# Copying k beside q[dst] out of PSUM, and making a block's products one block earlier, in a graph attention kernel on one core

## The chip, the core and the metric

The kernel runs on one core of a Trainium2 chip. The metric is the device time of one execution in microseconds; that of the kernel before is the median of three runs. The profile is of one further execution, whose own time is given beside its span.

## The reference, cut to what matters

One layer of attention over a graph's edges, with a layer norm ahead of it and a residual behind it. There are 12,500 nodes and 212,500 edges with 128 features each, sorted by destination, and 8 heads of 16.

```
h = maximum(layernorm(x), 0)
q = (h @ Wq.T + bq).reshape(N, 8, 16)
k = (edge_attr @ Wk.T + bk).reshape(E, 8, 16)
v = (h @ Wv.T + bv).reshape(N, 8, 16)
qs, qd = q[src], q[dst]
in_m, out_m, diag_m = sum(qs * k, -1), sum(qd * k, -1), sum(qs * qd, -1)
score = (segment_softmax(in_m / 4, dst) + segment_softmax(out_m / 4, dst)
         + segment_softmax(diag_m / 4, dst)) * edge_weight ** lam
out = x + leaky_relu(segment_sum(score[..., None] * v[dst], dst) @ Wo.T + bo, 0.1)
```

## The kernel before, in words

The edges are cut into blocks of 512, each of four times 128 edges (one edge to a partition). A block belongs to one of five strands s and to a group t; the loop of the main part (L1534 and following) runs over the 415 blocks g in the order s = g % 5, t = g // 5. All five engines have their own queue, and a helper, `pin`, ties each instruction to the one before it on its engine, so that every engine works in the order in which the program is written. That order is laid out by hand, and a late instruction holds up all that stands behind it on its engine.

What is done for a block g, with the line that does it:

- `gather` (L696, POOL): four indirect DMAs fetch the 512 rows q[src] into a tile qq. They are issued LOOK = 23 blocks ahead into QQ = 25 buffers. Each of the four is tied to a product of PE of the iteration before (`behind`), so that it does not start earlier.
- `one_hots` (L1177, L1178, ACT): from the places of the edges' destinations within a window of nodes, a one-hot matrix oh in bf16.
- `spread_q` (L1201, PE): four matmuls of oh with the window's rows of q and its rest, into kq_ps, a PSUM tile of 128x1024 floats with two buffers. One half becomes q[dst]; the other half takes a first term of k (the bias).
- `turn` (L1183, PE, and L1185, ACT): transposes the edge features into eT_ps (one buffer), and ACT copies them to eT in SBUF.
- `project` (L1190, PE, and L1194, ACT): multiplies eT by Wk and adds it onto k's half of kq_ps; then ACT copies the half with q[dst], 128x512, into qd in SBUF.
- `logits` (L1215, L1216, L1220, DVE): the product of qd with k (one input in SBUF, one in PSUM), the products of qq with both halves of kq_ps (again one in PSUM), and behind the blocks of s = 0, 2 and 4 a reduce over each head.

So kq_ps goes free when DVE's second product has read it, and the next but one block's `spread_q` on PE needs that buffer. In iteration g, PE and ACT make block g + 1's `spread_q` and `project`, block g + 2's `turn` and block g + 3's `one_hots`, and DVE makes block g's `logits`.

Once a group, spread over the five iterations, stands the softmax along each strand: scans on DVE (L1274, L1279, L1292), transposes on PE (L1241, L1366), powers (L1376 on DVE, an exponential L1377 on ACT, L1387 on DVE), the selection of rows (L1402 on PE, L1405 and L1406 on ACT) and the sums onto rows (L1417 on PE, L1423 on ACT). Node work and further terms of q (L1097 to L1148, L1305 to L1321) are put between. SP issues the loads: the edge features of a group (`fetch_edges`, ea, 1.28 MB) at s = 0 for the group after, the places (relb, L641) at s = 2 and the far rows (L627) at s = 3, each for the group after the next, window rows (L650) and the stores of sums (L1434).

Outside the loop, L861 and L958 belong to the start, where the q rows and the order of the edges are made, and ends_ab is a tile for the last sums at the tail.

Of the kernel before, what the change touches and what calls it, by code (L numbers as in the profile page):

```python
# [7 lines left out]
F32 = mybir.dt.float32  # L8
# [464 lines left out]
def ordered_path(ctx: ExitStack, tc: tile.TileContext, flag, x, src, dst, edge_attr, edge_weight,  # L473
# [19 lines left out]
    nc = tc.nc  # L493
    N, F = x.shape
    E = src.shape[0]
    P = 128
    NI = -(-N // P)
    NP = P * NI
    BE, JN = 512, 4
# [11 lines left out]
    H3 = 3 * HEADS  # L511
# [75 lines left out]
    worst = consts.tile([RW, 1], F32, name="worst")  # L587
    LEAD, RAW, AHEAD = 3, 15, 11
    raw_i = consts.tile([P, LEAD, S, JN], I32, name="raw_i")
    LOOK, QQ, BEGIN = 23, 25, 12  # L590
    end = S * G
    edges = ctx.enter_context(ExitStack())
    gath = edges.enter_context(tc.tile_pool(name="gath", bufs=QQ))
# [4 lines left out]
    def pin(inst):  # L598

        engine = str(inst.ins.engine)  # L600
        if engine in pinned:
            tc.add_manual_dep(inst.ins, pinned[engine], mybir.DependencyInfo(
                mybir.DependencyClass.NoSync, mybir.DependencyReason.DATA), reason="in order")
        pinned[engine] = inst.ins.name
        return inst
# [8 lines left out]
    qqs, st, eas, behind, base_v, places = {}, {}, {}, {}, {}, {}  # L614
# [124 lines left out]
    with tc.tile_pool(name="prep", bufs=1) as prep, \  # L739
# [44 lines left out]
        rest = E - (RW - 1) * RC  # L784
# [280 lines left out]
    class Nodes:  # L1065
# [39 lines left out]
        def turn(self, to):  # L1105
            for b in range(self.n):
                pin(nc.tensor.transpose(to[:, b, :], self.h[:, b, :], ident))
            if self.hT is None:
                self.hT = fin.tile([P, JN, P], F32, name="hT")
            pin(nc.scalar.copy(self.hT[:, :self.n], to[:, :self.n]))  # L1110
# [50 lines left out]
    with tc.tile_pool(name="work", bufs=2) as work, \  # L1161
            tc.tile_pool(name="scan", bufs=2) as scan, \
            tc.tile_pool(name="ps", bufs=1, space=PSUM) as ps:
        kqs, eTs, qds, ohs, lTs, prods = {}, {}, {}, {}, {}, {}

        def banks_of(g):

# [4 lines left out]
        def one_hots(g):  # L1172

            if g < end:
                oh = ohs[g] = work.tile([K3, BE], BF, name="oh", bufs=5)
                d = places[g // S][:K3, g % S, :]
                pin(nc.scalar.activation(d, d, AF.Abs, bias=before[:K3]))  # L1177
                pin(nc.scalar.activation(oh, d, AF.Relu, bias=1.0, scale=-1.0))  # L1178
# [9 lines left out]
        def project(g):  # L1188
            for j in range(JN):
                pin(nc.tensor.matmul(kqs[g][:, j, 1, :], eTs[g][:, j, :], wk, start=False,  # L1190
                                     stop=(j % 2 == 1)))
            del eTs[g]
            qds[g] = work.tile([P, JN, F], F32, name="qd")
            pin(nc.scalar.copy(qds[g], kqs[g][:, :, 0, :]))  # L1194

        def spread_q(g):

            s, win = g % S, st[g // S]["win"]
            kq = banks_of(g)
            for j in range(JN):  # L1200
                pin(nc.tensor.matmul(kq[:, j].rearrange("p i f -> p (i f)"),  # L1201
                                     ohs[g][:, j * P:(j + 1) * P], win[:, s:S + 1:S - s, :],
                                     start=(j % 2 == 0), stop=False))
            del ohs[g]

        def logits(g):
            s, t = g % S, g // S
            if s == 0:
                lTs[t] = scan.tile([P, JN, S, H3], F32, name="lT", bufs=3)
            alone = t == G - 1 and s > 2  # L1210
            lo = s if alone else max(0, s - 1 + s % 2)
            if s == lo:
                prods[0] = work.tile([P, JN, 2, 3, F], F32, name="prod", bufs=1)
            prod = prods[0][:, :, s - lo]
            pin(nc.vector.tensor_mul(prod[:, :, 2, :], qds[g], kqs[g][:, :, 1, :]))  # L1215
            pin(nc.vector.tensor_mul(prod[:, :, 0:2, :],  # L1216
                                     qqs[g][:, :, None, :].to_broadcast([P, JN, 2, F]),
                                     kqs[g]))
            if s % 2 == 0 or alone:
                pin(nc.vector.tensor_reduce(  # L1220
                    lTs[t][:, :, lo:s + 1, :].rearrange("p j s c -> p j (s c)"),
                    prods[0][:, :, :s + 1 - lo].rearrange("p j s i (h d) -> p j (s i h) d", d=DIM),
                    AX.X, ALU.add))
            del kqs[g], qds[g], qqs[g]

        last = {}
        ends_ab = scan.tile([P, len(rest) * JN, 2, 2 * H3], F32, name="ends_ab", bufs=1)
        for i in range(2):
            ends_t.append(scan.tile([K4, P], BF, name=f"ends_t{i + 2}", bufs=1))
            nc.vector.memset(ends_t[-1][0:1, :], 1.0)  # L1230
# [1 line left out]
        def small(shape, name):  # L1232
            return ps.tile(shape, F32, name=name, tag="small", bufs=3)
# [286 lines left out]

        products = str(mybir.EngineType.PE)
        leaving, last_pair = pairs[G - 3], pairs[G - 1]
        fetch_rows(0)
        fetch(1)
        fetch_places(1)
# [5 lines left out]
        turn(1)  # L1531
        one_hots(1)
        one_hots(2)
        for g in range(end):  # L1534
            s, t = g % S, g // S
            nodes_before(t, s)
            gather(g + LOOK)
            if s == 0:
                fetch_edges(t + 1)
            if g + 1 < end:  # L1540
                spread_q(g + 1)
                behind[g + 1, 0] = pinned[products]
                project(g + 1)
                behind[g + 1, 1] = pinned[products]
            if g + 2 < end:
                turn(g + 2)
                behind[g + 1, 2] = pinned[products]
            if s == 4:
                later(weigh_powers, t - 2)
            logits(g)  # L1550
            if s == 3:
                later(powers, t - 2)
            one_hots(g + 3)
            if s == 0:
                if t > 0:
                    turn_logits(t - 1)
                later(select, t - 2)
                later(spread_far, t - 2)
            elif s == 1:
                later(scan_on, t - 1)  # L1560
                later(scan_back, t - 2)
                if t == 1:
                    logits_few()
            elif s == 2:
                if t == G - 2:
                    show_ends(G - 1)
# [12 lines left out]
            if t == G - 3 and 0 < s < 3:  # L1579
                select(G - 2 + s)  # L1580
            if t == G - 2 and s == 4:
                show_ends(G)
            if t == G - 1 and s == 0:
                select(G - 2)
            if t == G - 1 and s == 4:
                show_ends(G - 2)
            behind[g + 1, 3] = pinned[products]
            nodes_between(t, s)
            other_terms(t, s)
            if g == 12 * S:  # L1590
                examine()
            begin_rest(g - (end - BEGIN))
            if g == end - 2:
                hold(rest[0], True)
            if g == end - 1:
                last_pair.turn(small([P, JN, P], "node_ps"))
                more_banks()
            if g < S:
                of = [u for u in range(NU) if g in parts_of(u)]
                pin(nc.scalar.dma_start(  # L1600
                    sums[g][of[0] * UN:(of[0] + len(of)) * UN].rearrange(
                        "(n p) i c -> p n (i c)", p=P),
                    blank[:, None, :].to_broadcast([P, 2 * len(of), 2 * 2 * H3])))
# [28 lines left out]
        hold(rest[1])  # L1632
        last_pair.turn(small([P, JN, P], "node_ps"))
        last_pair.project_o(small([P, JN, F], "node_ps"))
        for r, of in enumerate(rest):
            of.load_sums(ends_ab[:, r * JN:r * JN + of.n], of.more)
        last_pair.take_larger()
# [88 lines left out]
```

## Time and profile before

| what | value |
|---|---|
| median of 3 runs | 2659.78 us (2658.79 to 2670.84) |
| the profiled execution's own time | 2642.74 us |
| its span | 2640.9 us |
| mean granted clock of PE | 0.786 |
| DMA, mean over the span | 135 GB/s |

In the profile, PE is the matmuls, PEld the weight loads beside them, DVE, ACT, POOL and SP the other engines. A group of instructions is given by line, engine, operation, and "out<-in" by the tiles' names, with how often it ran, its busy time, the mean of one in ns, and the idle time of its engine in front of it with what ended that. "Issue" is idle time in which the engine waited for nothing that the profile shows; "remote" is a releaser that it cannot name. A row of the list of waits has the total in us, how often, and the longest. A row of the timeline has the start and the duration in us, and in brackets the idle time before it. The matmuls' ends are modelled.

### The profile page before, as it was taken

The numbers are of one execution on the slowest core, as the hardware profiler recorded it, in microseconds if no ns is written. First come the engines' busy times: TensorE is split into PE (matmuls) and PEld (weight loads), VectorE is DVE, ScalarE is ACT, GpSimd is POOL, SyncE is SP. The second block draws the span as 40 slices with busy tenths as digits, with TensorE's granted clock in tenths as the row PEclk, the third lists the DMA queues.
The fourth block names the chain that finished last, engine by engine and source line by source line (L and its number), as shares of the span: only waits on it lengthen the run. The fifth ranks groups of instructions, "written<-read, shape, count | busy, mean of one in ns | idle before, by whom it ended". The sixth has DMA issues, their size and how long they took to land.

```text
span 2640.9 us, 34648 instructions
## 1 busy us (share of the span) xinstructions
PE 1657.0 (63%) x9986; PEld 1406.9 (53%) x9986; DVE 2002.2 (76%) x2205; ACT 1422.5 (54%) x2742; POOL 1587.3 (60%) x1678
## 2 busy tenths in 40 slices
PE   5655656565665566666666666565666666666677
PEld 4544545454555455555555565454555555555665
DVE  6656777777787777777878777777877787778896
ACT  6644555455555555555555555555554555555572
POOL 6666666666666666666666666666666666666200
PEclk9876777778777887877878777878877787778786
DMA  8464444444444444444444444444444444444431
GB/s 235 143 202 130 132 121 121 145 131 121 129 147 132 131 132 148 140 132 130 134 139 144 126 134 144 144 122 130 146 139 129 124 145 139 120 126 133 122 91 53
DMA packets 306303, 355.74 MB, mean 135 GB/s; under 512 B 118433, under 2 KB 225899, under 8 KB 305795
## 3 DMA queue, kind: packets, MB, share of 16 engines
q1 hardware_dynamic: 238340, 238.99, 29.8%
q0 software_dynamic: 53184, 108.92, 15.0%
q10 hardware_dynamic: 14580, 5.53, 0.8%
q8 instruction: 82, 1.34, 0.2%
q14 instruction: 117, 0.96, 0.1%
HBM read 321.41 MB, written 31.85 MB: 134 GB/s over the span
## 4 chain that ended last, share of the span: by engine, by line
PE 31%; ACT 22%; another core or an unknown queue 17%; issue 14%; DVE 10%; DMA 0%; DVEq 0%; POOL 0%; ACTq 0%; SPq 0%; POOLq 0%
PE kq_ps L1190 11%; PE w_ps L1417 6%; PE kq_ps L1201 5%; ACT qd L1194 4%; ACT eT L1185 4%; PE eT_ps L1183 4%; ACT relb L1177 4%; DVE lT L1220 3%; DVE prod L1216 3%; ACT oh L1178 2%; PE node_ps L1115 2%; ACT sel L1406 2%; ACT sel L1405 2%; ACT back L1377 1%
## 5 line engine op out<-in xcount | busy, mean ns | idle before, releaser
L696 POOL DMA_INDIRECT qq<-q_table,src_i x1600 | 1517.2, 948 | 852.1 <-issue 368.8
L1190 PE MATMUL kq_ps<-wk,eT 128*128 128x128 f32 x3320 | 627.3, 348 | 677.0 <-ACT eT L1185 478.3
L1190 PEld LDWEIGHTS kq_ps<-wk,eT 128*128 128x128 f32 x3320 | 554.3, 252 | 757.7 <-ACT eT L1185 526.3
L1220 DVE TENSOR_REDUCE lT<-prod 128x192 f32<-128x3072 f32 (+1 forms) x250 | 702.3, 2809 | 8.5
L1194 ACT COPY qd<-kq_ps 128x512 f32<-128x512 f32 x415 | 242.0, 583 | 723.2 <-remote 443.9
L1216 DVE TENSOR_TENSOR prod<-qq,kq_ps 128x1024 f32<-128x1024 f32 x415 | 504.0, 1214 | 0.0
L1215 DVE TENSOR_TENSOR prod<-qd,kq_ps 128x512 f32<-128x512 f32 x415 | 283.1, 682 | 179.5 <-issue 97.5
L1201 PE MATMUL kq_ps<-win,oh 114*128 114x256 bf16 x1660 | 296.5, 307 | 96.8 <-issue 44.5
L1185 ACT COPY eT<-eT_ps 128x512 f32<-128x512 f32 x415 | 244.5, 589 | 174.8 <-remote 117.0
L1183 PE MATMUL eT_ps<-ident,ea 128*128 128x128 f32 x1660 | 321.4, 329 | 5.6 <-issue 5.6
L1177 ACT ACTIVATE relb<-relb,before 114x512 bf16<-114x512 bf16 x415 | 301.8, 727 | 0.0
L1201 PEld LDWEIGHTS <-oh 114*128 114x128 bf16 x1660 | 178.1, 111 | 172.6 <-issue 136.8
L1178 ACT ACTIVATE oh<-relb 114x512 bf16<-114x512 bf16 x415 | 261.5, 630 | 13.2
L1183 PEld LDWEIGHTS eT_ps<-ident,ea 128*128 128x128 f32 x1660 | 258.8, 175 | 6.2 <-issue 6.2
L1417 PE MATMUL w_ps<-back,sel 128*114 128x144 f32 (+1 forms) x1312 | 208.6, 323 | 72.4 <-ACT sel L1406 52.7
L1387 DVE TENSOR_TENSOR back<-back,m_ps 128x480 f32<-128x480 f32 x84 | 54.9, 653 | 256.1 <-ACT back L1377 239.3
L1417 PEld LDWEIGHTS w_ps<-back,sel 128*114 128x114 f32 x1312 | 194.3, 219 | 99.4 <-ACT sel L1406 72.7
L1274 DVE TENSOR_TENSOR_SCAN u<-far,u,l_ps 120x512 f32<-120x512 bf16 x82 | 104.5, 1275 | 30.0 <-PE kq_ps L1201 12.4
L1292 DVE TENSOR_TENSOR_SCAN m<-far_ps,head,u 120x512 f32<-120x512 f32 x81 | 103.9, 1282 | 8.4
L1423 ACT COPY rows<-w_ps 114x240 f32<-114x240 f32 x84 | 29.8, 355 | 129.1 <-PE kq_ps L1201 43.3
L696 POOL DMA_INDIRECT qq<-in_x_dram,raw_i x60 | 61.5, 1024 | 35.7 <-issue 15.6
L1366 PE MATMUL m_ps<-ident,m 120*128 120x120 f32 x332 | 70.1, 351 | 5.5 <-DVE m L1292 2.8
(196 smaller groups left out, 1458.8 us busy)
## 6 DMA issues: line engine op xcount, KB each, us to landing
ea<-in_edge_attr_dram SPq DMA_DIRECT2D x83, 1280.0 KB
relb<-rel_d SPq DMA_DIRECT2D x83, 640.0 KB
qq<-q_table,src_i POOLq DMA_INDIRECT x1600
win<-q_table SPq DMA_DIRECT2D x415, 28.5 KB
far<-far_d SPq DMA_DIRECT2D x84, 120.2 KB
q_table<-more_q SPq DMA_DIRECT2D x40, 192.0 KB
sums<-rows SPq DMA_DIRECT2D x408, 7.1 KB
q_table<-xq SPq DMA_DIRECT2D x24, 256.0 KB
```

The lines of the kernel that those rows point to most:

```text
L696: rows = pin(nc.gpsimd.indirect_dma_start(out=qq[:, j, :], out_offset=None, in_=x if g < RAW else q_table, in_offset=bass.IndirectOffsetOn ...
L1177: pin(nc.scalar.activation(d, d, AF.Abs, bias=before[:K3]))
L1178: pin(nc.scalar.activation(oh, d, AF.Relu, bias=1.0, scale=-1.0))
L1183: pin(nc.tensor.transpose(eT_ps[:, j, :], eas[g // S][:, g % S, j * F:(j + 1) * F], ident))
L1185: pin(nc.scalar.copy(eT, eT_ps))
L1190: pin(nc.tensor.matmul(kqs[g][:, j, 1, :], eTs[g][:, j, :], wk, start=False, stop=(j % 2 == 1)))
L1194: pin(nc.scalar.copy(qds[g], kqs[g][:, :, 0, :]))
L1201: pin(nc.tensor.matmul(kq[:, j].rearrange("p i f -> p (i f)"), ohs[g][:, j * P:(j + 1) * P], win[:, s:S + 1:S - s, :], start=(j % 2 == 0), ...
L1215: pin(nc.vector.tensor_mul(prod[:, :, 2, :], qds[g], kqs[g][:, :, 1, :]))
L1216: pin(nc.vector.tensor_mul(prod[:, :, 0:2, :], qqs[g][:, :, None, :].to_broadcast([P, JN, 2, F]), kqs[g]))
L1220: pin(nc.vector.tensor_reduce(lTs[t][:, :, lo:s + 1, :].rearrange("p j s c -> p j (s c)"), prods[0][:, :, :s + 1 - lo].rearrange("p j s i ...
L1417: pin(nc.tensor.matmul(w_ps[:, own[0]:own[-1] + 1, :].rearrange("p s c -> p (s c)"), d["sel"][:n, j, lo:lo + TRIO, :].rearrange("p s w -> ...
```

## The change

`project` no longer copies the half with q[dst] alone: ACT copies the whole of kq_ps, 128x1024, into an SBUF tile kq with three buffers. Both products of `logits` then read kq, so all their inputs are in SBUF, and kq_ps goes free when ACT's copy is through. The work ahead is moved by one block: iteration g makes `spread_q` and `project` of block g + 2, `turn` of g + 3 and `one_hots` of g + 4, and one of each more stands before the loop. `fetch_edges(1)` is issued before the loop, ahead of the first window rows, and in the loop the edges of the group after the next at s = 3. For room in SBUF the gathers look 22 blocks ahead with 24 buffers, and ends_ab at the tail takes the products' buffer. The number of instructions of each engine stays the same.

```diff
-    LOOK, QQ, BEGIN = 23, 25, 12
+    LOOK, QQ, BEGIN = 22, 24, 12
...
-            qds[g] = work.tile([P, JN, F], F32, name="qd")
-            pin(nc.scalar.copy(qds[g], kqs[g][:, :, 0, :]))
+            held_kq[g] = work.tile([P, JN, 2, F], F32, name="kq", bufs=3)
+            pin(nc.scalar.copy(held_kq[g], kqs.pop(g)))
...
-            pin(nc.vector.tensor_mul(prod[:, :, 2, :], qds[g], kqs[g][:, :, 1, :]))
+            kq = held_kq.pop(g)
+            pin(nc.vector.tensor_mul(prod[:, :, 2, :], kq[:, :, 0, :], kq[:, :, 1, :]))
             pin(nc.vector.tensor_mul(prod[:, :, 0:2, :],
-                                     qqs[g][:, :, None, :].to_broadcast([P, JN, 2, F]),
-                                     kqs[g]))
+                                     qqs[g][:, :, None, :].to_broadcast([P, JN, 2, F]), kq))
...
+        fetch_edges(1)
         fetch_rows(0)
...
+        spread_q(1)
+        project(1)
+        turn(2)
+        one_hots(3)
         for g in range(end):
             s, t = g % S, g // S
             nodes_before(t, s)
             gather(g + LOOK)
-            if s == 0:
-                fetch_edges(t + 1)
-            if g + 1 < end:
-                spread_q(g + 1)
+            if s == 3:
+                fetch_edges(t + 2)
+            if g + 2 < end:
+                spread_q(g + 2)
                 behind[g + 1, 0] = pinned[products]
-                project(g + 1)
+                project(g + 2)
                 behind[g + 1, 1] = pinned[products]
-            if g + 2 < end:
-                turn(g + 2)
+            if g + 3 < end:
+                turn(g + 3)
                 behind[g + 1, 2] = pinned[products]
...
-            one_hots(g + 3)
+            one_hots(g + 4)
```

How the order of an engine changes is seen at two places. On ACT, in the steady loop at iteration s = 3 (qd and kq are the copies out of kq_ps, back the exponential, sel the selection of rows), before:

```order
L1194 COPY qd<-kq_ps 128x512
L1185 COPY eT<-eT_ps 128x512
L1377 ACTIVATE back<-back 128x20x24
L1177 ACTIVATE relb<-relb,before 114x512
L1178 ACTIVATE oh<-relb 114x512
L1405 ACTIVATE sel<-d_ps 128x380 x2
```

and after:

```order
L1194 COPY kq<-kq_ps 128x1024
L1185 COPY eT<-eT_ps 128x512
L1376 ACTIVATE back<-back 128x20x24
L1177 ACTIVATE relb<-relb,before 114x512
L1178 ACTIVATE oh<-relb 114x512
L1404 ACTIVATE sel<-d_ps 128x380 x2
```

The sequence is the same; the copy is twice as wide, it belongs to a block that is one later, and the exponential stands behind it as before. On DVE, where s = 3 passes into s = 4 (prod is the products' buffer, back the powers, lT the reduced logits), before:

```order
L1376 TENSOR_TENSOR back<-lT,m_ps 128x20x24
L1319 TENSOR_TENSOR more_q<-more_q,more_q_6409 128x256
L1387 TENSOR_TENSOR back<-back,m_ps 128x20x24
L1215 TENSOR_TENSOR prod<-qd,kq_ps 128x4x128
L1216 TENSOR_TENSOR prod<-qq,kq_ps 128x4x256
L1220 TENSOR_REDUCE lT<-prod 128x4x48
```

and after:

```order
L1375 TENSOR_TENSOR back<-lT,m_ps 128x20x24
L1318 TENSOR_TENSOR more_q<-more_q,more_q_6424 128x256
L1386 TENSOR_TENSOR back<-back,m_ps 128x20x24
L1216 TENSOR_TENSOR prod<-kq 128x4x128
L1217 TENSOR_TENSOR prod<-qq,kq 128x4x256
L1220 TENSOR_REDUCE lT<-prod 128x4x48
```

DVE's order stands as it was; what has changed is that neither product reads PSUM any more.

More of the change, by code (lines that the diff above doesn't have):

```diff
@@ L1163, in ordered_path @@
             tc.tile_pool(name="ps", bufs=1, space=PSUM) as ps:
-        kqs, eTs, qds, ohs, lTs, prods = {}, {}, {}, {}, {}, {}
+        kqs, eTs, held_kq, ohs, lTs, prods = {}, {}, {}, {}, {}, {}
         def banks_of(g):
@@ L1223, in logits @@
                     AX.X, ALU.add))
-            del kqs[g], qds[g], qqs[g]
+            del qqs[g]
         last = {}
-        ends_ab = scan.tile([P, len(rest) * JN, 2, 2 * H3], F32, name="ends_ab", bufs=1)
         for i in range(2):
@@ L1634, in ordered_path @@
         last_pair.project_o(small([P, JN, F], "node_ps"))
+        ends_ab = work.tile([P, JN, 2, 3, F], F32, name="prod", bufs=1).rearrange(
+            "p j s i f -> p (j s i f)")[:, :len(rest) * JN * 4 * H3].rearrange(
+            "p (n i c) -> p n i c", i=2, c=2 * H3)
         for r, of in enumerate(rest):
```

## The prediction

> **What bounds the kernel now.** I read the page first: the share of each engine and the chain that ended last.
>
> ```profile
> span 2640.9 us, 34648 instructions
> PE 1657.0 (63%) x9986; PEld 1406.9 (53%) x9986; DVE 2002.2 (76%) x2205; ACT 1422.5 (54%) x2742; POOL 1587.3 (60%) x1678
> PE 31%; ACT 22%; another core or an unknown queue 17%; issue 14%; DVE 10%; DMA 0%; DVEq 0%; POOL 0%; ACTq 0%; SPq 0%; POOLq 0%
> PE kq_ps L1190 11%; PE w_ps L1417 6%; PE kq_ps L1201 5%; ACT qd L1194 4%; ACT eT L1185 4%; PE eT_ps L1183 4%; ACT relb L1177 4%; DVE lT L1220 3%; DVE prod L1216 3%; ACT oh L1178 2%; PE node_ps L1115 2%; ACT sel L1406 2%; ACT sel L1405 2%; ACT back L1377 1%
> ```
>
> No engine is full. DVE, the busiest, is a tenth of the chain; PE and ACT are half of it, and 17% is a releaser that the profile cannot name ("remote" in the waits). Next came the table by stage: a stretch of the steady loop, and one near the end in which hardly any gather is left.
>
> ```profile
> core 0: us, PE busy (x) PEld busy (x) DVE busy (x) ACT busy (x) POOL busy (x), PEclk, DMA share, GB/s
> 600.00:1200.00 600.00, 368.88 (x2290) 312.37 (x2290) 462.45 (x436) 321.77 (x609) 385.61 (x408) 0.80 0.46 135
> 2480.00:2560.00 80.00, 56.89 (x372) 49.07 (x371) 75.89 (x70) 58.18 (x115) 1.68 (x4) 0.85 0.35 105
> ```
>
> In 600 us POOL starts 408 gathers, four to a block, so 102 blocks pass: 5.88 us a block, 29.4 us a group of five. DVE works 77% of that. Without gathers DVE is busy 95% of the time (75.89 of 80): there the kernel is bound by DVE, and with gathers by something else. The list of waits says by what.
>
> ```profile
> PE kq_ps L1190 <- ACT eT L1185: 478.3, 152, 8.4
> ACT qd L1194 <- remote: 443.9, 101, 12.3
> POOL qq L696 <- issue: 384.3, 1232, 3.4
> DVE back L1387 <- ACT back L1377: 239.3, 65, 8.5
> POOL qq L696 <- remote: 222.7, 149, 2.7
> PE kq_ps L1201 <- DVE prod L1216: 42.9, 49, 3.0
> ```
>
> PE waits for ACT's copy of eT, ACT waits in front of its copy of qd for "remote", and DVE waits for an exponential queued on ACT behind that copy. PE waits for DVE's products, which is what the change takes away, for 42.9 us only. One such hold, from the timeline:
>
> ```profile
> 1358.39 0.95 POOL L696 DMA_INDIRECT qq<-q_table,src_i  x1 [0.30 <-issue]
> 1358.81 1.06 PE L1190 MATMUL kq_ps<-wk,eT 128*128 128x128 f32 x8
> 1359.64 0.94 POOL L696 DMA_INDIRECT qq<-q_table,src_i  x1 [0.30 <-issue]
> 1360.89 0.95 POOL L696 DMA_INDIRECT qq<-q_table,src_i  x1 [0.30 <-issue]
> 1362.14 0.95 POOL L696 DMA_INDIRECT qq<-q_table,src_i  x1 [0.30 <-issue]
> 1364.64 0.59 ACT L1194 COPY qd<-kq_ps 128x512 f32<-128x512 f32 x1 [3.57 <-remote]
> 1364.87 0.95 POOL L696 DMA_INDIRECT qq<-q_table,src_i  x1 [1.78 <-remote]
> 1365.76 1.57 PEld L1190 LDWEIGHTS kq_ps<-wk,eT 128*128 128x128 f32 x7 [4.77 <-ACT eT L1185]
> 1366.24 0.66 DVE L1387 TENSOR_TENSOR back<-back,m_ps 128x480 f32<-128x480 f32 x1 [4.72 <-ACT back L1377]
> ```
>
> PE's projection is through at 1359.87, yet the copy that needs nothing else of this block starts at 1364.64. POOL meanwhile runs one gather every 1.25 us up to 1363.09, then itself waits for a product of PE, and goes on 0.23 us after ACT's copy begins. ACT and POOL are let go together, 1.55 us after POOL ran dry. I read this as: PE's finished products are not seen while POOL works through a run of gathers, so POOL's gathers pace the loop. A group holds 20 gathers of 1.25 us, 25.0 of the 29.4 us; the other 4.4 are POOL's waits. That is inferred from when the releases fall; the releaser is not in the trace.
>
> **The change part by part.** The rows for the prices:
>
> ```profile
> L696 POOL DMA_INDIRECT qq<-q_table,src_i x408 | 386.6, 948 | 214.7 <-issue 94.1 <-remote 52.5 <-PE kq_ps L1201 25.8
> L1194 ACT COPY qd<-kq_ps 128x512 f32<-128x512 f32 x415 | 242.0, 583 | 723.2 <-remote 443.9 <-PE kq_ps L1201 96.4 <-PE kq_ps L1190 63.7
> L1405 ACT ACTIVATE sel<-d_ps 128x380 f32<-128x380 f32 x164 | 69.7, 475 | 0.1
> L1406 ACT ACTIVATE sel<-sel 128x760 f32<-128x760 f32 x82 | 68.6, 837 | 2.6
> L1215 DVE TENSOR_TENSOR prod<-qd,kq_ps 128x512 f32<-128x512 f32 x415 | 283.1, 682 | 179.5 <-issue 97.5 <-ACT qd L1194 68.0 <-DVE lT L1220 0.9
> L1216 DVE TENSOR_TENSOR prod<-qq,kq_ps 128x1024 f32<-128x1024 f32 x415 | 504.0, 1214 | 0.0
> L1319 DVE TENSOR_TENSOR more_q<-more_q,more_q 128x256 f32<-128x256 f32 x40 | 16.8, 419 | 5.7 <-issue 4.4 <-ACT more_q L1317 1.4
> ```
>
> *The copy of 1024 instead of 512.* From 380 to 512 elements ACT's price rises by 583 - 475 = 108 ns, 0.82 ns an element; from 380 to 760 by 362 ns, 0.95. So 512 more cost 0.42 to 0.49 us; I take 0.42, since its two rows read PSUM as this copy does. Times 415 that is 174 us of ACT. The copy of qd is on the chain for 4% of 2640.9 = 106 us of its 242.0, or 44%; at that share 76 us lie on the path, between 0 (under a hold) and 203 us (all of it, at 0.49).
>
> *DVE's two products read only SBUF.* Their own length: L1319 has both inputs in SBUF and takes 419 ns for 256. Between 512 and 1024 elements the price is (1214 - 682) / 512 = 1.04 ns, and 419 + 256 x 1.04 = 685, against 682 now. So nothing, 0.
>
> What they do to POOL is another matter. The timeline where gathers meet DVE operations of that kind:
>
> ```profile
> 139.69 2.28 DVE L861 SCALAR_TENSOR_TENSOR of<-dst_r 104x2048 bf16<-104x2048 int32 x1
> 140.90 1.90 POOL L696 DMA_INDIRECT qq<-q_table,src_i  x1 [0.30 <-issue]
> 741.99 0.94 POOL L696 DMA_INDIRECT qq<-q_table,src_i  x1 [0.30 <-issue]
> 743.21 0.42 DVE L1319 TENSOR_TENSOR more_q<-more_q,more_q 128x256 f32<-128x256 f32 x1
> 743.24 1.20 POOL L696 DMA_INDIRECT qq<-q_table,src_i  x1 [0.30 <-issue]
> ```
>
> The gather that starts inside L1319 ends 0.81 us after that operation (744.44 against 743.63), and the one inside L861 0.83 us after it (142.80 against 141.97). Both behave as if they had begun when DVE was done. L1216 with one input in PSUM leaves them alone: in the hold above, the gather of 1358.39 begins beside it and takes its usual 0.95. The Trainium skill ("SBUF — State Buffer", section "Who interferes with whom") has this as a rule: a DVE instruction with two SBUF inputs contends with a GpSimd instruction that reads SBUF, because the second input comes through a shared read interface. The rows above agree. The same section remarks, as an inference, that descriptor generation needs only the write interface; by that the gathers would be spared, this term would be nothing and the time that of the first rival, 2693. The 1.20 and 1.90 speak against it.
>
> The price: L1215 and L1216 take 1.90 of 5.88 us. A gather that starts at a random moment falls into the first with 0.682 / 5.88 and then loses half of it, 0.341, and into the second with 1.214 / 5.88 and loses 0.607: 0.040 + 0.125 = 0.165 us. Four to a block, 400 blocks with gathers: 264 us of POOL time. If a gather caught by the first product is also kept out by the second, it is 1.90 x 1.90 / 2 / 5.88 = 0.307 us each, 491 us. The lower end is 0, if gathers fall between the products.
>
> *PE waits for the copy instead of the products.* L1201's 42.9 us go. What PE waits for next is the same ACT copy in the hold, which it has met 152 times already. DVE's wait for the exponential (239.3) stays: that stands on ACT behind the copy that is held, and the lead does not move it.
>
> *One block more of lead.* Same counts on every engine; spread, project, turn and one-hots stand in the same order within an iteration, so ACT's copies still stand between PE's projections. The four extra pieces before the loop are taken off its end: 0. Gathers look 22 ahead instead of 23, still four groups: 0. A projected block waits in a third SBUF buffer; DVE can be about one block later before anybody feels it.
>
> *The load of edges* (1.28 MB, SP) goes ahead of the first window loads, and then from s = 0 to s = 3 of the group before, between the places and the far rows. In the loop it is earlier than needed, so 0; at the start it takes 1.28 MB off the window loads. At the 185 GB/s that the first 150 us show (below) that is 6.9 us if all of it is late; 0 to 7, taken 0, since PE's first blocks wait for the q rows.
>
> ```profile
> 0.00:150.00 150.00, 95.91 (x522) 79.35 (x522) 100.05 (x390) 98.72 (x242) 95.51 (x101) 0.85 0.66 185
> ```
>
> *ends_ab in the products' buffer* is at the tail, after the last reduce: 0.
>
> **The sum.** If POOL paces the loop, a longer copy lies mostly in the time in which gathers run, and the sum is 264 - 43 = +221 us. The profiled run took 2642.74 us (2640.9 span and 1.8 around it), 17 below the median of 2659.78; its sum is 2864, and I set the difference onto the median: 2881, say 2880 us.
>
> **The rivals.**
>
> *POOL's waits swallow the lost time; ACT's copy is the price.* POOL idles 214.7 us in 600, of which 408 x 0.30 = 122 are issue, so it really waits 92 us, 0.90 a block; the gathers lose 0.66 a block. If these waits simply shrink, POOL costs nothing, and what is left is +76 - 43 = +33: 2693. For it: 0.66 is under 0.90. Against it: a wait is there because POOL ran dry, and it seems to be what lets PE's products be seen.
>
> *Faster: DVE's place in the chain goes.* The 3% of lT and the 3% of prod are 158 us; if the third buffer frees PE of all of it and the copy keeps its 76, that is -82: 2578. If the copy hides too, 2502. This decides if holds are jitter that a block of lead bridges, so that DVE runs through them; from a hold below about 5.9 us, one block, it can. For it: DVE has 24% idle and reaches 95% once gathers end. Against it: DVE's largest wait is not for the products but for the exponential.
>
> *Hidden altogether.* The holds end when they end, copy and gathers fit within them: -43 to 0, 2617 to 2660, taken 2655.
>
> **How the numbers follow.** POOL paced 0.43; swallowed, copy on the path 0.23; faster 0.23; hidden 0.11. About 0.5%, 13 us, is what can be told from no change. Slower: 0.43 and 0.19 of the second case (all but its lower edge): 0.62. Same: the other 0.04 and 0.08 of the hidden case: 0.12. Faster: 0.23 and 0.03: 0.26. The range goes from 2590, into the faster case but not to its 2578, to 2960, above 2659.78 + 264 = 2924 for hand-over in some blocks but not all (491). It leaves out some 0.14 of the faster case and 0.06 above.
>
> The likeliest case's own range is 2750 to 2960: its lower end is hand-over at 1.23 us a block, less the 0.90 of POOL's waits, 0.33 x 400 = 131, less 43.
>
> **What would show it.** The copy at L1194 should read about 1.00 us, the two products 0.68 and 1.21. The mean gather should rise from 948 ns to about 1113 (948 + 165), with rows of 1.2 to 2.0 where one starts inside a product; if it stays at 948, the forecast's first step is wrong. If it rises and the loop still needs 29.4 us a group, POOL does not pace it, and POOL's idle must have shrunk by as much. PE's wait at L1201 for DVE should be gone. If DVE's idle falls well below 24% and the wait for the exponential shrinks, the lead bridges the holds, and it is faster.

## The result, and the profile after

The changed kernel takes 2686.91 us (median of 6 runs, 2681.63 to 2691.06) against 2659.28 us (median of 6, 2655.03 to 2670.84): a ratio of 1.0098, with a 95% interval of 1.0073 to 1.0122. So it is 1% slower. The forecast was 2880, in a range of 2590 to 2960. Its first rival, in which POOL's waits swallow the lost time and the copy's price is left, gave 2693.

One thing has to be known for all that follows: chips differ. On the chip of this measurement, and on one of the chips of the experiments, the kernel before takes 2639 to 2660 us and the profiles show the waits for an unnamed releaser; on the four other chips it takes 2161 to 2164 us and the profiles show next to none (2.7 us at most). I speak of chips with holds and without; each chip was met at one time only, so it may be the chip or its condition at that time. Each run is compared with the kernel before on its own chip.

From the groups of the page after: the gathers, the copy, and the two products (columns as before: busy time, mean of one in ns, idle time ahead of it).

```profile
span 2688.3 us, 34107 instructions
L696 POOL DMA_INDIRECT qq<-q_table,src_i x1600 | 1689.2, 1056 | 733.2 <-issue 385.1
L1194 ACT COPY kq<-kq_ps 128x1024 f32<-128x1024 f32 x415 | 418.9, 1009 | 740.7 <-remote 506.2
L1217 DVE TENSOR_TENSOR prod<-qq,kq 128x1024 f32<-128x1024 f32 x415 | 505.6, 1218 | 0.0
L1216 DVE TENSOR_TENSOR prod<-kq 128x512 f32<-128x512 f32 x415 | 284.2, 685 | 31.6 <-ACT kq L1194 14.6
L1201 PE MATMUL kq_ps<-win,oh 114*128 114x256 bf16 x1660 | 296.7, 308 | 10.5 <-issue 8.4
```

The prices of the single operations came out as forecast: the copy at 1.01 us (1.00), the products at 685 and 1218 ns (685 and unchanged). PE's wait at L1201 for the products is gone. The gathers are longer, 1056 instead of 948 ns, which is two thirds of the forecast 165 ns: 172 us of POOL's time and not 264. But of the 172 only a part is in the time, since POOL's idle time shrank by 118.9 us, from 852.1 to 733.2.

The table by stage, in the same 600 us of the loop:

```profile
600.00:1200.00 600.00, 358.56 (x2262) 303.07 (x2262) 447.70 (x423) 357.65 (x601) 422.86 (x400) 0.78 0.45 131
```

There are 400 gathers instead of 408, so 30.0 us a group instead of 29.4. Over 80 groups that is the 47 us by which the two profiled spans differ (2688.3 against 2640.9). With 0.30 us of issue for each gather taken off, POOL waits 600 - 422.9 - 120 = 57 us there, where it waited 92.

The list of waits after:

```profile
ACT kq L1194 <- remote: 506.2, 112, 12.5
PE kq_ps L1190 <- ACT eT L1185: 421.9, 144, 13.7
DVE back L1386 <- ACT back L1376: 180.8, 42, 9.3
POOL qq L696 <- remote: 161.6, 145, 2.9
PE kq_ps L1190 <- ACT kq L1194: 79.8, 32, 7.8
ACT eT L1185 <- remote: 75.2, 58, 4.0
```

The holds are as large as they were: ACT waits for the unnamed releaser 506.2 + 75.2 = 581 us, against 443.9 + 117.0 = 561 before (the 117.0 is of eT's copy, in its row of before).

```profile
L1185 ACT COPY eT<-eT_ps 128x512 f32<-128x512 f32 x415 | 244.5, 589 | 174.8 <-remote 117.0 <-PE kq_ps L1201 20.1 <-issue 17.9
```

And a hold can end while POOL works. From the timeline after:

```profile
1354.42 1.38 POOL L696 DMA_INDIRECT qq<-q_table,src_i  x1 [0.30 <-issue]
1356.10 0.94 POOL L696 DMA_INDIRECT qq<-q_table,src_i  x1 [0.30 <-issue]
1357.35 0.94 POOL L696 DMA_INDIRECT qq<-q_table,src_i  x1 [0.30 <-issue]
1358.59 0.95 POOL L696 DMA_INDIRECT qq<-q_table,src_i  x1 [0.30 <-issue]
1359.56 1.01 ACT L1194 COPY kq<-kq_ps 128x1024 f32<-128x1024 f32 x1 [5.52 <-remote]
1359.85 0.94 POOL L696 DMA_INDIRECT qq<-q_table,src_i  x1 [0.30 <-remote]
```

POOL goes from gather to gather with 0.30 us between them, and ACT's copy, held for 5.52 us, starts 0.02 us behind the end of a gather, with the next one to follow at its usual 0.30. In the prediction's example POOL had run dry 1.55 us before the release, and I took that for the cause. One example does not decide it. Before the change ACT's copies of qd and eT wait for more than 1 us on the unnamed releaser 141 times: 115 of these holds end while POOL is dry, 26 while it goes from gather to gather. After it there are 137: 81 and 56, and 47 of these end inside a gather.

What ends a hold can be found in the traces as recorded, which also keep the semaphore updates, the signals by which an engine tells the others that a piece of work is done. All 141 held copies before and all 137 after start within 0.06 us after an update of PE's own semaphore. In the prediction's example five of PE's updates come together, from 1364.61 to 1364.81, while the matmuls that they belong to end in the trace from 1359.87 to 1361.27. So the unnamed releaser is PE, whose signals come late. The matmuls' ends are modelled, so the trace does not tell whether the products were late too.

### The profile page after: what moved, and what is told of

The parts are those of the page before. It is cut to its first block, busy times and chain, and to the rows that moved or that the text cites. A ratio compares the mean times of both kernels' runs of the same rounds, so it can differ in the third digit from the quotient of the medians.

```text
span 2688.3 us, 34107 instructions
## 1 busy us (share of the span) xinstructions
PE 1641.6 (61%) x9986; PEld 1377.6 (51%) x9986; DVE 2004.2 (75%) x2205; ACT 1591.6 (59%) x2742; POOL 1758.5 (65%) x1678
## 4 chain that ended last, share of the span: by engine, by line
PE 31%; ACT 26%; another core or an unknown queue 18%; issue 14%; DVE 8%; POOL 1%; DMA 1%; SPq 0%; ACTq 0%; DVEq 0%; POOLq 0%
PE kq_ps L1190 11%; ACT kq L1194 8%; PE w_ps L1416 6%; PE kq_ps L1201 4%; ACT eT L1185 4%; ACT relb L1177 4%; PE eT_ps L1183 3%; DVE lT L1220 2%; DVE prod L1217 2%; ACT oh L1178 2%; ACT sel L1404 2%; ACT sel L1405 2%; PE node_ps L1115 1%; PE m_ps L1365 1%
## 5 line engine op out<-in xcount | busy, mean ns | idle before, releaser
L696 POOL DMA_INDIRECT qq<-q_table,src_i x1600 | 1689.2, 1056 | 733.2 <-issue 385.1
L1190 PE MATMUL kq_ps<-wk,eT 128*128 128x128 f32 x3320 | 617.2, 344 | 801.3 <-ACT eT L1185 421.9
L1190 PEld LDWEIGHTS kq_ps<-wk,eT 128*128 128x128 f32 x3320 | 539.3, 246 | 896.1 <-ACT eT L1185 472.2
L1194 ACT COPY kq<-kq_ps 128x1024 f32<-128x1024 f32 x415 | 418.9, 1009 | 740.7 <-remote 506.2
L1217 DVE TENSOR_TENSOR prod<-qq,kq 128x1024 f32<-128x1024 f32 x415 | 505.6, 1218 | 0.0
L1216 DVE TENSOR_TENSOR prod<-kq 128x512 f32<-128x512 f32 x415 | 284.2, 685 | 31.6 <-ACT kq L1194 14.6
L1201 PE MATMUL kq_ps<-win,oh 114*128 114x256 bf16 x1660 | 296.7, 308 | 10.5 <-issue 8.4
L1185 ACT COPY eT<-eT_ps 128x512 f32<-128x512 f32 x415 | 244.8, 590 | 98.3 <-remote 75.2
L1386 DVE TENSOR_TENSOR back<-back,m_ps 128x480 f32<-128x480 f32 x84 | 54.8, 653 | 261.1 <-ACT back L1376 180.8
L1201 PEld LDWEIGHTS <-oh 114*128 114x128 bf16 x1660 | 175.1, 110 | 77.8 <-issue 40.7
L1375 DVE TENSOR_TENSOR back<-lT,m_ps 128x480 f32<-128x480 f32 x83 | 54.1, 651 | 132.4 <-issue 62.9
```

The lines of the kernel that those rows point to most:

```text
L696: rows = pin(nc.gpsimd.indirect_dma_start(out=qq[:, j, :], out_offset=None, in_=x if g < RAW else q_table, in_offset=bass.IndirectOffsetOn ...
L1185: pin(nc.scalar.copy(eT, eT_ps))
L1194: pin(nc.scalar.copy(held_kq[g], kqs.pop(g)))
L1216: pin(nc.vector.tensor_mul(prod[:, :, 2, :], kq[:, :, 0, :], kq[:, :, 1, :]))
L1217: pin(nc.vector.tensor_mul(prod[:, :, 0:2, :], qqs[g][:, :, None, :].to_broadcast([P, JN, 2, F]), kq))
```

## The experiments

The theories: "gathers", that the loss comes from gathers which DVE's products lengthen; "copy", that it is the copy's added 0.42 us in front of PE's next projection; "lead", that it comes with the block of lead; and "swallowed" against "one to one", on what becomes of POOL's lost time under holds.

### The parts of the change, one at a time, on a chip without holds

The wide copy alone: no lead, and DVE reads k from PSUM.

```diff
-            pin(nc.vector.tensor_mul(prod[:, :, 2, :], kq[:, :, 0, :], kq[:, :, 1, :]))
+            pin(nc.vector.tensor_mul(prod[:, :, 2, :], kq[:, :, 0, :], k_ps[:, :, 1, :]))
             pin(nc.vector.tensor_mul(prod[:, :, 0:2, :],
-                                     qqs[g][:, :, None, :].to_broadcast([P, JN, 2, F]), kq))
+                                     qqs[g][:, :, None, :].to_broadcast([P, JN, 2, F]), k_ps))
```

> Without the lead, ACT copies all 1024 elements, but DVE reads only q[dst] from the copy and k from PSUM as before. The copy takes 1.01 us (it did after) and the gathers 0.95. Theory 'copy' (the 27 us are the copy's added 0.42 us where it lies between PE's projections): 2690 to 2735, since the copy's share of the chain and PE's waits for DVE's products are both there. Theory 'gathers' (the 27 us come from gathers that DVE's products make longer): 2650 to 2668, no change. If it is slower than the change itself, the lead or the earlier release of PSUM gives something back.

Measured: 2166.66 against 2163.52 us, ratio 1.0009 (1.0000 to 1.0018). The wide copy costs 3 us or nothing.

Both products from SBUF, still without the lead (the loop's lines as before the change, two buffers for kq):

```diff
-            if g + 2 < end:
-                spread_q(g + 2)
+            if g + 1 < end:
+                spread_q(g + 1)
```

> As the run before, but both products read the copy in SBUF, so kq_ps goes free with ACT's copy and gathers meet DVE on the port: mean gather about 1.04 to 1.11 us instead of 0.95. Still no lead. Theory 'copy': equal to the run with the wide copy alone or up to 40 us below it (PE's waits for the products go). Theory 'gathers': 25 to 60 us above the run with the wide copy alone. Against the changed kernel it gives what the block of lead is worth: theory 'copy' says 0 to 30 us of gain by the lead.

Measured: 2384.02, ratio 1.1005 (1.0988 to 1.1022), 217 us above the run before it, where theory "gathers" had 25 to 60. The only steps between these two are the products' second input and who frees kq_ps. The gathers of the first and then of the second, from their pages:

```profile
L696 POOL DMA_INDIRECT qq<-q_table,src_i x1600 | 1519.2, 950 | 488.0 <-issue 260.1
```

```profile
L696 POOL DMA_INDIRECT qq<-q_table,src_i x1600 | 1737.7, 1086 | 487.9 <-issue 288.2
```

POOL's busy time rises by 218.5 us, the time by 217.4; its idle time stays at 488, which is 0.30 us for each of 1600 gathers. POOL runs gathers without a pause here, and what a gather loses the kernel loses.

The change with a copy of 512 (k's half is left out; both products read q[dst] in its place):

```diff
-            held_kq[g] = work.tile([P, JN, 2, F], F32, name="kq", bufs=3)
-            pin(nc.scalar.copy(held_kq[g], kqs.pop(g)))
+            held_kq[g] = work.tile([P, JN, F], F32, name="kq", bufs=3)
+            pin(nc.scalar.copy(held_kq[g], kqs.pop(g)[:, :, 0, :]))
```

> The changed kernel with a copy of 512 elements: k's half is left out, and both products read q[dst] in its place from SBUF, so shapes, ports and lead are as in the change. ACT's copy 0.58 us. Theory 'copy': 2600 to 2655, at least 30 us below the changed kernel. Theory 'gathers': 2675 to 2695, as the changed kernel, with the mean gather still at 1.05.

And the change with the wide copy moved behind that of eT on ACT:

```diff
                 turn(g + 3)
                 behind[g + 1, 2] = pinned[products]
+            if g + 2 < end:
+                hold_kq(g + 2)
```

> The changed kernel, but ACT copies eT of block g + 3 ahead of kq of block g + 2, so PE's next projection does not stand behind the wide copy; the lead leaves DVE a block of time for it. Theory 'copy': at or below the kernel before, 2600 to 2660. Theory 'gathers': 2675 to 2700, no change against the changed kernel. A danger for both: eT's copy waits for the transposes that follow the projection on PE, so kq starts some 0.6 us later.

Measured: 2350.70, ratio 1.0855 (1.0837 to 1.0872), and 2353.12, ratio 1.0873 (1.0855 to 1.0891). The absolute times expected were for a chip with holds and all missed. What counts is that neither the copy's width nor its place moves the time.

### Both kernels again

> The kernel before, once more, with a profile. In the four runs so far it took 2163 us on their chip and not the 2659 us of the first measurement, and the wide copy alone showed no wait for an unnamed releaser. Theory 'holds' (the first measurement was made under a condition in which PE's products were seen late, 3 to 5 us at a time, while gathers ran, and that condition comes with the chip): either about 2163 us with no unnamed releaser in front of ACT's copies, or about 2650 with some 400 to 500 us of it. A mixture would speak against it.

> The changed kernel, once more. Theory 'gathers': without the holds it takes 2340 to 2360 us, as with the narrow copy or the copy behind eT, some 8.7% above the kernel before, and POOL's busy time is 170 to 195 us above; with the holds 2680 to 2695, 1% above. Theory 'copy': without the holds it is above the run with the narrow copy (2351) by 30 us or more.

Measured: 2168.39 us for the one run of the kernel before (2162.20 median of its 7 runs beside it), and 2352.04 for the change, ratio 1.0876 (1.0831 to 1.0921), within 2 us of the two runs above. The gathers before and after on that chip:

```profile
span 2166.5 us, 34648 instructions
L696 POOL DMA_INDIRECT qq<-q_table,src_i x1600 | 1517.1, 948 | 487.6 <-issue 255.3
```

```profile
span 2349.1 us, 34107 instructions
L696 POOL DMA_INDIRECT qq<-q_table,src_i x1600 | 1708.0, 1067 | 487.7 <-issue 271.6
L1217 DVE TENSOR_TENSOR prod<-qq,kq 128x1024 f32<-128x1024 f32 x415 | 506.2, 1220 | 192.1 <-DMA qq<-q_table,src_i 104.3
```

And two of the waits of the kernel before there:

```profile
ACT qd L1194 <- PE kq_ps L1190: 315.4, 188, 6.0
PE kq_ps L1201 <- DVE prod L1216: 312.1, 222, 5.6
```

ACT waits for PE by name and not for an unnamed releaser, and PE waits 312.1 us for DVE's products, the wait that the change takes away. It is gone after (L1201 is idle 2.6 us in all) and nothing is gained. POOL's time rises by 190.9 us, the medians by 189.8. DVE now stands 192.1 us in front of its second product, 104.3 of it for the gathered rows themselves: the stream of gathers has become the bound. Without holds the change costs 8.8%, all of it through the gathers. The block of lead takes 32 us off the run without it (2384 to 2352), and here too POOL says why: its gathers take 1067 instead of 1086 ns, 30 us over 1600.

### One product from SBUF, on a chip with holds

```diff
             kq, k_ps = held_kq.pop(g), kqs.pop(g)
+            pin(nc.vector.tensor_mul(prod[:, :, 2, :], kq[:, :, 0, :], k_ps[:, :, 1, :]))
             pin(nc.vector.tensor_mul(prod[:, :, 0:2, :],
                                      qqs[g][:, :, None, :].to_broadcast([P, JN, 2, F]), kq))
```

> The wide copy without the lead; the first product reads k from PSUM as before, only the second (1.21 us) has both inputs in SBUF. Theory 'gathers' (a gather that starts inside such a product ends about 0.82 us after it, and POOL's added time comes through one to one): mean gather 1.03 to 1.08, and 120 to 195 us above the kernel before, by as much as POOL's busy time rises; between the run with the wide copy alone (+3) and the one with both products (+220). A theory by which the early release of kq_ps by ACT, and not the port, makes the loss: no more than +20, since DVE's first product still holds kq_ps.

This run and the three that follow fell on a chip with holds. Measured: 2648.43 against 2639.11 us, ratio 1.0041 (1.0024 to 1.0059).

```profile
L696 POOL DMA_INDIRECT qq<-q_table,src_i x1600 | 1650.1, 1031 | 736.1 <-issue 385.7
ACT kq L1194 <- remote: 468.6, 105, 8.8
```

The gathers take 1031 ns, as expected, and lose 133 us against the 1517.2 of the first profile; but the time rises by 9 us, where 120 to 195 were expected. So under holds the mechanism is there and the passing on is not. The run was meant to tell the two SBUF inputs from the early release of kq_ps as the cause of the longer gathers. The time cannot, since under holds either would give little, but the trace can, for it has products of both kinds side by side:

```profile
1208.04 0.69 DVE L1216 TENSOR_TENSOR prod<-kq,kq_ps 128x512 f32<-128x512 f32 x1
1208.18 0.94 POOL L696 DMA_INDIRECT qq<-q_table,src_i  x1 [0.30 <-issue]
1208.65 1.22 DVE L1217 TENSOR_TENSOR prod<-qq,kq 128x1024 f32<-128x1024 f32 x1
1209.43 1.26 POOL L696 DMA_INDIRECT qq<-q_table,src_i  x1 [0.30 <-issue]
```

The gather that starts inside the first product (one input in PSUM) takes its usual time; the one inside the second (both in SBUF) ends 0.82 us after it. Over the whole trace, the 263 gathers that start inside a first product take 0.95 us in the mean, the 353 inside a second 1.32, and the 984 others 0.95. So it is the second SBUF input and not the early release.

The run also bounds the wide copy without the lead under holds: with longer gathers beside it, the whole is 9 us.

### Holds made by hand

To have holds where I wanted them, ACT copies 16 small pieces of the finished kq_ps into a spare tile, at s = 1 and s = 3, ahead of its copy:

```diff
+            if g % S in (1, 3):
+                spare = work.tile([P, F], F32, name="spare", bufs=1)
+                for i in range(16):
+                    pin(nc.scalar.copy(spare, kqs[g][:, i % JN, 0, :]))
```

> The kernel before with a hold made by hand, to have on this chip what the first measurement had: at s = 1 and s = 3 ACT copies 16 times a piece of 128x128 of the finished kq_ps into a spare tile ahead of qd, some 4.3 us each time. The output stays as it was. The gathers should stay at 0.95 us. 2350 to 2700 us: the hold lies between PE's projections, POOL runs dry and waits some 2 to 6 us a group.

> The changed kernel with the same hold by hand. Against the kernel before with the hold: theory 'swallowed' (POOL's lost time is used up by the waits that a hold gives it): 0 to 70 us slower though the gathers take 1.04 to 1.07 us, so a ratio of 1.00 to 1.03. Theory 'one to one': 150 to 200 us slower, as without the hold.

> The changed kernel with a copy of 512 (k's half left out, q[dst] read twice) and the same hold by hand. Theory 'copy' (under holds what is left of the loss is the copy's 0.42 us behind each hold and between PE's projections): 30 to 110 us below the changed kernel with the hold, at or below the kernel before with it. Theory 'gathers': as the changed kernel with the hold, within 15 us.

The chip already had holds of its own. Measured, against the same 2639.11: the kernel before with them 2730.22, ratio 1.0345 (1.0310 to 1.0381); the change 2809.54, ratio 1.0646 (1.0596 to 1.0695); the change with the narrow copy 2738.18, ratio 1.0392 (1.0354 to 1.0429). From the pages, the kernel before with holds by hand, the change, and the narrow copy:

```profile
L696 POOL DMA_INDIRECT qq<-q_table,src_i x1600 | 1514.3, 946 | 923.1 <-issue 375.3
```

```profile
ACT spare L1196 25%; PE kq_ps L1190 14%; ACT kq L1198 10%; ACT eT L1185 5%; ACT relb L1177 4%; PE kq_ps L1205 3%; PE eT_ps L1183 3%; ACT oh L1178 3%; PE w_ps L1420 2%; ACT sel L1409 2%; ACT sel L1408 2%; ACT back L1380 1%; PE m_ps L1369 1%; ACT far_ps L1288 1%
L696 POOL DMA_INDIRECT qq<-q_table,src_i x1600 | 1679.6, 1050 | 834.1 <-issue 370.6
```

```profile
L696 POOL DMA_INDIRECT qq<-q_table,src_i x1600 | 1684.0, 1053 | 756.4 <-issue 376.1
```

With the narrow copy the gathers lose 169.7 us, POOL's idle time falls by 166.7, and the kernel is 8 us slower: swallowed, nearly to the last. The wide copy then adds 71 us, with the gathers at the same 1050 ns. Of the copy's 174 us that is 41%, close to the 44% that the prediction took from the chain, and the copy has 10% of the chain. Here "copy" holds, though the narrow copy was to end at or below the kernel before with the same holds, not 8 us above it. For the change itself, 79 us above that kernel, I had given 0 to 70 and missed by 9; for the kernel before with them I had given 2350 to 2700, and 2730 is above that.

These three runs are no picture of the chip's own holds, though. The hand-made ones did not come on top of them but took their place: ACT's waits for the unnamed releaser in front of the copies out of kq_ps and eT_ps are 523 us in the run with one product from SBUF, on this chip, and 30, 72 and 129 us here (kernel before, change, narrow copy). In their stead ACT works on the pieces, 704 us in the first of the three. It is busy for 77 to 81% of the span and carries 46 to 56% of the chain, against 59% and 26% after the change alone. What a longer copy costs where ACT is the bound need not be what it costs where ACT waits for PE.

### The first four again, and the change without gathers

To see copy and lead apart under the chip's own holds, four runs were made once more, and then three of them again. Both times they fell on chips without holds.

> The wide copy without the lead, products from PSUM, meant for a chip in which the kernel before takes about 2640 to 2660 us (the holds are there; on the others it was +3 us). Theory 'copy': +40 to +80. Theory 'lead': the 27 us of the first measurement come with the block of lead, which lets PE and ACT run ahead into holds, and the copy alone is +0 to +10.

> Both products from SBUF, no lead. Under holds, theory 'swallowed': the gathers still take 1.05 us or more, but this is within 30 us of the run with the wide copy alone, where it was +220 without holds. Theory 'one to one': +150 or more. Theory 'lead': below the changed kernel, at +10 or so; theory 'copy': at or above the changed kernel, +27 or more.

> The changed kernel with a copy of 512 (k left out, q[dst] read twice). Under holds, theory 'copy': 30 us or more below the changed kernel, so at 0 or faster than the kernel before; the hand-made holds showed 71 us between the two. Theory 'lead': as the changed kernel, +20 to +30.

> The changed kernel with eT copied ahead of the wide copy. Under holds, theory 'copy': the copy no longer stands in front of PE's next projection, so 30 to 70 us below the changed kernel, at or below the kernel before. Theory 'lead': no change against the changed kernel, +20 to +30.

> Both products from SBUF, no lead, once more for a chip with holds (the kernel before at 2640 to 2660 us). With one product from SBUF and the wide copy it was +9 us there. Theory 'lead' (the 27 us come with the block of lead): +10 to +20, below the changed kernel. Theory 'copy': +25 or more, since the copy is as wide. Theory 'one to one': +150 or more. Without holds +219, as before.

> The changed kernel with a copy of 512 (k left out, q[dst] read twice), for a chip with holds. Theory 'copy': 0 or faster than the kernel before, 25 us or more below the changed kernel. Theory 'lead': +20 to +30. Without holds +186, as before.

> The changed kernel with eT copied ahead of the wide copy, for a chip with holds. Theory 'copy': at or below the kernel before. Theory 'lead': +20 to +30. Without holds +189, as before.

Measured: the wide copy alone 1.0013 (1.0004 to 1.0023); both products from SBUF 1.1013 (1.0995 to 1.1032) and 1.1020 (1.0995 to 1.1045); the narrow copy 1.0862 (1.0841 to 1.0884) and 1.0880 (1.0853 to 1.0908); the copy behind eT 1.0880 (1.0861 to 1.0898) and 1.0886 (1.0862 to 1.0909). They repeat the first four to 0.3% and leave their own question open.

The last run stops the gathers after 22 blocks; all later blocks read those rows of q[src] again.

```diff
-        if g < end:
+        if LOOK <= g < end:
+            qqs[g] = qqs[LOOK - 1 - (g - LOOK) % 2] if g < LOOK + 2 else qqs[g - 2]
+        elif g < end:
```

> The changed kernel whose gathers stop after the first 22 blocks (all later blocks read those rows of q[src] again, so 88 of the 1660 gathers of the edges are left). Theory 'gathers pace the loop': 2000 to 2100 us in either condition, bound by DVE at 95% busy or more in the loop, with the unnamed releaser gone from the waits also on a chip that shows holds: the copy and the lead cost nothing by themselves. If it stays above 2160, something other than the gathers is slow in the change; if a chip with holds still shows them, they do not come with the gathers.

Measured: 2158.98 against 2160.96, ratio 0.9993 (0.9982 to 1.0004). Its chain:

```profile
DVE 57%; ACT 16%; PE 12%; issue 7%; DMA 5%; SPq 1%; ACTq 0%; DVEq 0%
```

Without its gathers the changed kernel takes as long as the kernel before with them, so what the change loses on such a chip comes with the gathers. That the rest of the change costs nothing at all is not quite shown, since the kernel before was not run without gathers. There is little room for it: between 600 and 1200 us DVE is busy for 571 us in the kernel before on a chip without holds, and for 567 us here. The expected 2000 to 2100 was wrong. With the gathers out of the way DVE carries the chain, at 94% busy in the loop. So on such a chip DVE and the gathers are nearly equal bounds, and little was left for a block of lead to gain. No run points to a version that beats the kernel before.

## Why the prediction was wrong

**What bounds the kernel.** I read "PE's finished products are not seen while POOL works through a run of gathers, so POOL's gathers pace the loop". This is the step that failed on the chip measured. The gathers lost 172 us there and the time rose by 28; with one product from SBUF 133 and 9, with hand-made holds and the narrow copy 170 and 8. A loop that POOL paces would have risen by all of it, and on the chips without holds it did (191 and 190, 218 and 217). Half of the reading was right: PE's signals do come late. But they do not wait for POOL to run dry: 56 of the 137 holds after the change ended while it went from gather to gather, 47 of them inside one, and the holds' sum stayed where it was (561 and 581 us) while POOL had less idle time. What fits is that the hold paces, POOL waits for it, and a longer gather takes its time out of that wait. Why the signals are late is open.

**The gathers' price.** The mechanism was right: gathers that start inside a product with two SBUF inputs end some 0.82 us after it. The Trainium skill's rule ("SBUF — State Buffer", "Who interferes with whom": a DVE instruction with two SBUF inputs contends with a GpSimd instruction that reads SBUF) agrees with the pair of runs at 950 and 1086 ns. Its remark in the same section, marked there as inferred, that descriptor generation needs the write interface would have left the gathers alone if they needed nothing else; the 1086 ns speak against that. The size was too large: 264 us against 172 under holds and 191 without. The share that starts inside a product was right: 567 of the 1600 in the profile after, or 35%, against 1.90 / 5.88 = 32%. So was the first product's term: 221 gathers at 1.22 us, which is 0.038 us over all gathers, against 0.040. The second product's is the one that was off: 346 gathers at 1.27 us, 0.070 against 0.125. The working took them to start at random moments, but 189 of the 346 start in the last 0.12 us of the product and lose nothing. The rows give a reason: a gather caught by the first product ends 0.82 us after it, and 0.30 us later, 1.12 us into a second product of 1.22, the next one starts. The other 1033 gathers take 0.95 us as before.

**The copy.** The length was right (1009 ns). What of it lies on the path depends on where it is asked: 3 us or nothing without holds, 71 of 174 us with hand-made holds, where ACT is the bound. In the sum I had dropped it, on the ground that it lies in the time in which gathers run; the rival that came nearest has it at 76. Under the chip's own holds one run bears on it, the one with one product from SBUF: the wide copy is in it, PE's wait for the products is 17.0 us instead of 42.9, and by the rival's working it should have been some 76 - 26 = 50 us slower. It was 9 us slower.

**Products and lead.** PE's wait for the products went, as said. DVE's wait for the exponential did not go, 239.3 to 180.8 us, and L1386's idle time as a whole stayed at 261 us (256 before), for the reason given: the exponential stands behind the held copy.

**The rival that came nearest** set the lost time of POOL against its waits (0.66 against 0.90 us a block). Both numbers were in the text, and I gave it 0.23. That part of it came true. By its working, +76 - 43 = +33; measured +28. That the sum came so near is in part luck, since the run just named speaks against its 76. How these 28 us divide between the copy under the chip's own holds, what is left of the gathers' loss, and the lead, is open: the runs that would tell did not fall on a chip with holds. The chain after gives the copy 8%, which is 215 us, where it had 4%, 106 us; that speaks for the copy and does not prove it.

```profile
PE kq_ps L1190 11%; ACT kq L1194 8%; PE w_ps L1416 6%; PE kq_ps L1201 4%; ACT eT L1185 4%; ACT relb L1177 4%; PE eT_ps L1183 3%; DVE lT L1220 2%; DVE prod L1217 2%; ACT oh L1178 2%; ACT sel L1404 2%; ACT sel L1405 2%; PE node_ps L1115 1%; PE m_ps L1365 1%
```

## What to carry to other kernels

Moving an operand of a DVE product from PSUM to SBUF does not change DVE's own time, but it can hold up a stream of gathers on POOL: cost it at that engine, and then ask whether POOL has waits that would take it up. Two events that end together do not show which releases which: compare the loss with the slack of the engine that loses, and if the slack is larger, start from "swallowed". A mean hides how gathers and products fall: count the gathers that start inside a product, and compare their length with that of the others. A wait for an unnamed releaser in the one trace at hand may belong to the chip and not to the kernel.

## What the runs showed of the hardware that was not expected

The same kernel takes 2161 to 2164 us on four chips and 2639 to 2660 on the one measured first and on one more. The difference goes with holds such as those of 3.57 and 5.52 us shown above, 444 to 506 us in front of one ACT copy alone (three profiles), in which ACT waits on after the trace has PE's product finished and starts when PE's signal comes, late and often with several others; on the other chips that copy waits for PE by name. Why some chips show this was not found. One more thing goes with it: the trace of the kernel before has 14,450 semaphore updates on the chip with holds and 45,484 on a chip without, so most of them are missing there. Whether the holds have to do with the recording of these signals was not tried. The price of the change goes with the kind of chip: 1.0% with holds, 8.8% without.
